# Making the constants out of the weights inside the first scan instead of ahead of the program

## The chip, the core and the metric

The kernel runs on one core of a Trainium2 chip. The core has five engines that run side by side, each through its own list of instructions in order: TensorE (PE, matmuls, with weight loads shown apart as PEld), VectorE (DVE), ScalarE (ACT), GpSimd (POOL) and SyncE (SP), which here only issues transfers. Transfers (DMAs) are issued from SP's queue and from ScalarE's queue and are moved by 16 DMA engines. The metric is the device time of one execution in microseconds (us); less is better. The time before is 4182.01 us, the median of 3 runs (4180.69 to 4185.67).

## The reference, cut to what matters

The input is `x`, 32 sequences of 256 tokens of 256 features. First a conditional state-space block, then two layers of local attention with a gated feed-forward, and the input is added at the end:

```python
xr, gate = split(x @ W_in.T, 2);  xr = xr + t_emb
xc = silu(causal_conv_4_taps(xr) + b_conv)                # 512 channels
xn = layernorm(xc) * ln_g + ln_b
Bm, Cm, dt = split(xn @ W_xproj.T, 3)                     # 16 states each
dt = tanh(dt @ W_dt.T + b_dt) * 0.01
Ad = 1 - dt * tanh(A_log);  Bd = Bm * minimum(norm(xn), 1)
# over the 256 tokens, one after the other:
h = clip(h * Ad + Bd (x) xn, -10, 10);  y = Cm . h
s = ((y + D * xn) * silu(gate)) @ W_out.T
# two layers, windows of 128 tokens, 8 heads of 64:
q, k = rotary(l2norm(q) * q_scale), rotary(l2norm(k) * k_scale)
s = s + attention(q, k, v) @ wo;  s = s + (a * gelu(g)) @ w2
out = x + s
```

Some constants depend on weights alone and not on `x`: the product of `W_dt` with the last third of `W_xproj`, that matrix times `ln_g`, sums of it over the channels (with `ln_g` and with `ln_b`, so that the layernorm can be applied after the projection), the rotary tables times `q_scale` and `k_scale`, half of `W_out`, `-0.01 * tanh(A_log)`, and small selection tables. A flag, `bounded`, says whether the largest `q_scale * k_scale` is so small that the softmax needs no maximum.

## The kernel before

The 32 sequences are worked in 4 groups of 8. `group_scan` is the state-space block of one group: 8 chunks of 32 tokens. Of a chunk it loads `xg`, projects it (`ps_in`, L330), adds the condition into `xr` (L360), applies the taps (`acc`, first on GpSimd at L366, the others on VectorE at L377) and the silu (`th` on ScalarE, L382, and `xc`, L387); projects to the states (`ps_raw`, L396, with `wx_sb`), transposes to tokens on the partitions (`tp_x`, L426), takes the layernorm's statistics (L436 to L446, with a power on GpSimd, L441), multiplies by `lng_sb` and adds `lnb_sb` on GpSimd (L457, L458), writes the rows to `xnd` in HBM (L462), and reads them back spread over the partitions (`xrep`, L547; for the first group half of them instead through `xq`, L602, and matmuls `bx`, L555). ScalarE scales them by `beta` (L566), and VectorE does one custom operation for each token, the recurrence `h` (L573). TensorE reads the states out (`y`, L585); then skip, gate, the projection with `w_out_sb` (L661), and the result goes to `ys` in HBM.

Every piece of this is put on an agenda by step: `at(s, piece, ...)`, where step `32*c + t` is token `t` of chunk `c`, and pieces of work ahead have smaller or negative steps. The order of emission follows the agenda; a scheduler in the framework may then move instructions within an engine's list by its own costs, unless one is marked to be kept in program order. A tile is taken from a pool by its tag, with a number of buffers; a new tile of a tag waits until the readers of the one that had the buffer are done.

`program` runs the scan of group 0 alone, then for each group the attention and feed-forward blocks of both layers, side by side with the scan of the next group. Its text is compiled twice, for both values of the flag; every engine loads `bounded` (L1318) and branches into one of them.

Ahead of the branch stands the setup. It is where the change works: all loads of constants on ScalarE's queue (L112, L119; only `w_in_sb` is on SP's), identity and masks, the halving of `w_out_sb` (L172), `head_rows` (L197), the tables `rc_sb` and `rs_sb` (L229), the flag (L237 to L244), the folding of `W_dt` into `wx` (`td`, `wdT`, L258 to L263), `wx_sb` (L265), and six times a `wide` copy on VectorE (L269) with four matmuls into `tw` (L272), whose sums are `wsum` and `wbias` (L279, L280).

## Time and profile before

| | us |
|---|---|
| median of 3 runs | 4182.01 |
| the profiled execution's own time | 4183.47 |
| its span in the profile | 4181.7 |
| TensorE busy | 3874.3 (93%) |
| VectorE busy | 2619.7 (63%) |
| ScalarE busy | 1742.8 (42%) |
| GpSimd busy | 1708.1 (41%) |

| stretch, us | what runs | length | TensorE | VectorE | ScalarE | GpSimd |
|---|---|---|---|---|---|---|
| 0 to 22.8 | loads, setup up to the flag | 22.80 | 1.55 | 6.58 | 1.49 | 3.31 |
| 22.8 to 37.2 | the rest of the setup | 14.40 | 12.43 | 4.33 | 0.00 | 0.28 |
| 37.2 to 70.7 | first chunk, up to the first `h` | 33.50 | 18.68 | 16.75 | 6.59 | 14.68 |
| 70.7 to 460 | the scan of group 0 alone | 389.30 | 367.77 | 326.23 | 210.07 | 142.74 |

The columns on the right are busy time in the stretch. A line of the timeline reads: start, duration, engine, line of the kernel, operation, the tile written, an arrow to the tiles read, shapes and types, how many records; in brackets how long the engine had been idle and what released it. SPq and ACTq are issues of transfers, not the transfers. A line of waits reads: engine and line that waited, for what, total us, how often, the longest. A float32 matmul leaves two records. A line of busy time by stretch reads: the stretch, its length, then PE, PEld, DVE, ACT and POOL busy with the number of instructions, the granted TensorE clock, DMA share and GB/s. TensorE's busy time is modelled at its ends, and a busy TensorE need not be at its peak.

### The profile page before, as it was taken

To read this page: it belongs to the slowest core of one execution; us is meant where nothing else is said; L and a number is where in the kernel's file an instruction comes from. 1 tells how busy PE (TensorE), PEld (TensorE's weight loads), DVE (VectorE), ACT (ScalarE), POOL (GpSimd) and SP (SyncE) were. 2 spreads that over 40 slices of the span, in tenths; PEclk is the share of its full clock that TensorE was granted. 3 is DMA by queue.
4 is the path that set the end of the run, shared out by engine and by line. 5 is a ranking of instruction groups with operands and counts; after the bars stand their busy time and mean duration, and the time that the engine had idled before them with its cause. 6 is when DMAs were issued, how large, how long until landed. Compare 5 with 4: busy or idle time off the path is not lost. (4 is left out here: it accounts for less than half of the span.)

```text
span 4181.7 us, 51837 instructions
## 1 busy us (share of the span) xinstructions
PE 3874.3 (93%) x18236; PEld 2002.1 (48%) x18236; DVE 2619.7 (63%) x4986; ACT 1742.8 (42%) x3217; POOL 1708.1 (41%) x1749
## 2 busy tenths in 40 slices
PE   6999899899988999899998999989998899999999
PEld 3333355444544455444455445544454545654653
DVE  5888467677766456766867636776776644434443
ACT  2555344444444334444544424444444533322331
POOL 3443265225543156423654136522454315513531
PEclk9999899999999999999999999999999999999999
DMA  3444213444335212344434421344433521000000
GB/s 123 121 124 119 58 44 95 113 117 112 91 87 139 81 43 77 111 110 111 116 86 114 121 65 44 81 126 111 118 91 84 142 78 37 3 19 22 1 11 31
DMA packets 257345, 353.09 MB, mean 84 GB/s; under 512 B 160867, under 2 KB 170420, under 8 KB 254900
## 3 DMA queue, kind: packets, MB, share of 16 engines
q1 hardware_dynamic: 172624, 337.67, 29.0%
q10 hardware_dynamic: 84452, 12.01, 1.8%
q8 instruction: 147, 2.41, 0.2%
q14 instruction: 122, 1.00, 0.1%
HBM read 314.49 MB, written 33.55 MB: 83 GB/s over the span
## 5 line engine op out<-in xcount | busy, mean ns | idle before, releaser
L573 DVE CUSTOM_DVE_ANT_0 h<-h,xrep,lim 128x512 f32<-128x512 f32 x1024 | 908.1, 887 | 94.8 <-PE y L585 36.0
L566 ACT ACTIVATE xrep<-xrep,beta 128x512 f32<-128x512 f32 x896 | 608.6, 716 | 793.3 <-DMA xrep<-xnd 732.8
L781 PE MATMUL ps_qkv<-wqkv_sb,res 128*128 128x512 f32 x1536 | 740.5, 621 | 28.4 <-ACT qT L825 6.6
L805 POOL TENSOR_TENSOR rot<-rot,swp 128x512 f32<-128x512 f32 x256 | 329.2, 1286 | 653.3 <-DVE swp L802 603.3
L781 PEld LDWEIGHTS ps_qkv<-wqkv_sb,res 128*128 128x128 f32 x1536 | 286.6, 196 | 381.9 <-issue 309.0
L813 POOL TENSOR_TENSOR rn<-ss,neg_half 128x8 f32<-128x8 f32 x256 | 437.4, 1708 | 21.6 <-DVE ss L811 9.7
L797 DVE TENSOR_TENSOR rot<-ps_qkv,rc_sb 128x512 f32<-128x512 f32 x256 | 175.6, 686 | 375.6 <-ACT sq L794 375.4
L330 PE MATMUL ps_in<-xg,w_in_sb 128*128 128x256 f32 x1024 | 398.4, 523 | 6.5 <-ACT pT L995 3.4
L1140 PE MATMUL po_f<-ag,w_sb 128*128 128x512 f32 (+1 forms) x768 | 356.0, 612 | 18.5 <-DVE ag L1121 18.5
L585 PE MATMUL y<-h,ly 128*32 128x512 f32 x2048 | 354.0, 639 | 11.3 <-DVE h L573 10.1
L1111 PE MATMUL pa<-hT,w_sb 128*128 128x512 f32 (+1 forms) x896 | 363.0, 595 | 0.0
L1121 DVE SCALAR_TENSOR_TENSOR ag<-pa,b_sb,gl 128x512 f32<-128x512 f32 x192 | 143.5, 747 | 317.9 <-PE pa L1111 166.2
L1111 PE MATMUL pg<-hT,w_sb 128*128 128x512 f32 x640 | 309.4, 606 | 0.0
L330 PEld LDWEIGHTS ps_in<-xg,w_in_sb 128*128 128x128 f32 x1024 | 194.1, 204 | 206.5 <-issue 125.2
L814 POOL TENSOR_TENSOR rot<-rot,rn 128x512 f32<-128x512 f32 x256 | 280.3, 1095 | 19.0
L377 DVE SCALAR_TENSOR_TENSOR acc<-xr,wc_sb,acc 128x256 f32<-128x256 f32 x384 | 199.2, 523 | 116.7 <-POOL acc L366 114.2
L1074 POOL TENSOR_TENSOR rstd<-ve,neg_half 128x1 f32<-128x1 f32 x128 | 75.8, 592 | 476.6 <-DVE ve L1072 466.1
L995 ACT ACTIVATE pT<-sc 128x512 f32<-128x512 f32 x384 | 206.3, 592 | 127.3 <-PE sc L986 113.7
L831 PE MATMUL ps_wo<-oT,wo_sb 128*128 128x256 f32 x1024 | 237.3, 385 | 0.0
L1140 PEld LDWEIGHTS po_f<-ag,w_sb 128*128 128x128 f32 (+1 forms) x768 | 135.1, 190 | 203.3 <-issue 138.7
L794 ACT ACTIVATE sq<-ps_qkv 128x512 f32<-128x512 f32 x256 | 148.8, 593 | 195.9 <-PE ps_qkv L781 148.1
L1111 PEld LDWEIGHTS pa<-hT,w_sb 128*128 128x128 f32 (+1 forms) x896 | 135.6, 170 | 189.3 <-issue 175.7
(151 smaller groups left out, 5592.9 us busy)
## 6 DMA issues: line engine op xcount, KB each, us to landing
xrep<-xnd SPq DMA_DIRECT2D x448, 512.0 KB
xnd<-xn SPq DMA_DIRECT2D x64, 256.0 KB
wqkv_sb<-in_wqkv_dram SPq DMA_DIRECT2D x8, 1536.0 KB
xd<-xnd SPq DMA_DIRECT2D x192, 64.0 KB
w_sb<-in_w_dram SPq DMA_DIRECT2D x8, 1364.0 KB
xg<-in_xT_dram SPq DMA_DIRECT2D x64, 128.0 KB
ys<-yo ACTq DMA_DIRECT2D x64, 128.0 KB
res<-ys SPq DMA_DIRECT2D x32, 256.0 KB
```

The source lines that it names most:

```text
L330: nc.tensor.matmul(ps, w_in_sb[:, k, ch * P : (ch + 1) * P], x, start=(k == 0), stop=(k == KM - 1),)
L566: nc.scalar.activation(bx, ck[c].pop(("bx", t), bx), AF.Copy, scale=ck[c]["beta"][:, t : t + 1])
L573: nc.vector._custom_dve(TENSOR_ADD_SAT, out=h_new, in0=state["h"], in1=bx, s0=ck[c]["lim"][:, 0, t : t + 1], s1=ck[c]["lim"][:, 1, t : t + 1],
L585: nc.tensor.matmul(ck[c]["y", hb][32 * q : 32 * q + 32, :], ly[hb % 2][:, 32 * t : 32 * t + 32], ck[c].pop(("h", hb * TB + t)), start=(i = ...
L781: nc.tensor.matmul(ps, res[b // 2][:, k, b % 2, t0 : t0 + W], wqkv_sb[:, k, a * DI : (a + 1) * DI], start=(k == 0), stop=(k == KM - 1),)
L805: nc.gpsimd.tensor_add(rot, rot, swp)
L813: nc.gpsimd.tensor_tensor(rn, ss, neg_half, ALU.pow)
L814: nc.gpsimd.tensor_mul(rot, rot, bc(rn, 2, DH))
L831: nc.tensor.matmul(po[:, d], wo_sb[:, c, d * P : (d + 1) * P], oT[:, c, :], start=(c == 0), stop=(c == NC_ - 1),)
L995: nc.scalar.activation(p, banks[r], AF.Exp)
L1111: nc.tensor.matmul(ps[0:n, :], self.w1[:, k, half_ * HID + o : half_ * HID + o + n], self.h[j][:, k].rearrange("p b t -> p (b t)"), start= ...
L1140: nc.tensor.matmul(self.po[d], self.w2[r0 : r0 + n, m, d * P : (d + 1) * P], self.ag[m][r0 : r0 + n, :], start=(m == 0), stop=(m == len(MC ...
```

## The change

The flag is computed first of all, from a load on SP's queue. The other constants made of weights go into `constants`, which `group_scan` calls for group 0 and which puts them on the agenda: the folding at steps -43 to -14, later loads at -16, the halving of `w_out_sb` at 14, tables from 50 on, `head_rows` from 100 on. The six `wide` copies, the halving, the tables (now four operations in place of eight) and `head_rows` are on GpSimd instead of VectorE, each marked to be kept at its place in program order. Temporary tiles come from the tags `rot` and `swp` of attention, and PSUM banks from the program's own pool. Both compiled programs contain them.

```diff
@@ -119,18 +119,26 @@
         nc.scalar.dma_start(out=t, in_=src)
         return t
+    bounded = const.tile([1, 1], I32, tag="bounded", name="bounded")
+    with tc.tile_pool(name="setup", bufs=1) as setup:
+        sq = setup.tile([1, L, 2, DH], FP, tag="sq", name="sq")
+        nc.sync.dma_start(out=sq, in_=qk_scale.unsqueeze(0))
+        nc.vector.tensor_mul(sq, sq, sq)
+        big = setup.tile([1, L, 2], FP, tag="big", name="big")
+        nc.vector.tensor_reduce(big, sq, AX.X, ALU.max)
+        nc.vector.tensor_mul(big[:, :, 0], big[:, :, 0], big[:, :, 1])
+        nc.vector.tensor_scalar(big[:, :, 1], big[:, :, 0], SCALES2, None, ALU.is_le)
+        allb = setup.tile([1, 1], FP, tag="allb", name="allb")
+        nc.vector.tensor_reduce(allb, big[:, :, 1], AX.X, ALU.min)
+        nc.vector.tensor_copy(bounded, allb)
     w_in_sb = loaded(w_inT, [P, KM, 2 * DI], "w_in_sb", nc.sync)
     cond_sb = loaded(condT, [P, NC_, B], "cond_sb")
     wc_sb = loaded(w_conv, [P, NC_, TAPS], "wc_sb")
     bconv_sb = loaded(b_conv, [P, NC_], "bconv_sb")
     lng_sb = loaded(s_ln_g.partition_broadcast(P), [P, DI], "lng_sb")
     lnb_sb = loaded(s_ln_b.partition_broadcast(P), [P, DI], "lnb_sb")
-    dskip_sb = loaded(d_skip.partition_broadcast(P), [P, DI], "dskip_sb")
-    w_out_sb = loaded(w_outT, [P, NC_, DM], "w_out_sb")
-    flg_sb = loaded(f_ln_g, [P, L, KM], "flg_sb")
-    flb_sb = loaded(f_ln_b, [P, L, KM], "flb_sb")
-    b1_sb = loaded(b1, [P, L, 2, len(MCH)], "b1_sb")
-    b2_sb = loaded(b2, [P, L, KM], "b2_sb")
     bdt_sb = per_state(b_dt, "bdt_sb")
     a_sb = per_state(a_log, "a_sb")
 
@@ -163,13 +171,6 @@
     nc.gpsimd.memset(neg_half, -0.5)
     half = const.tile([P, NJ], FP, tag="half", name="half")
     nc.gpsimd.memset(half, 0.5)
-    nc.scalar.activation(a_sb, a_sb, AF.Tanh)
-    nc.vector.tensor_scalar(a_sb, a_sb, -1.0, 0.01, ALU.mult, ALU.mult)
-    nc.vector.tensor_scalar(w_out_sb, w_out_sb, 0.5, None, ALU.mult)
 
@@ -192,19 +193,6 @@
     head_rows = const.tile([P, HEADS, DH], FP, tag="head_rows", name="head_rows")
     for r in range(2):
         nc.gpsimd.memset(head_cols[:, r, r * 16 : (r + 1) * 16], 1.0)
-    for h in range(HEADS):
-        row = 32 * (h // 2) + 16 * (h % 2)
-        nc.vector.tensor_copy(
-            head_rows[:, h, :], ident[:, row : row + 1].broadcast_to([P, DH])
-        )
...
     rc_sb = const.tile([P, L, NW, 2, DH], FP, tag="rc_sb", name="rc_sb")
     rs_sb = const.tile([P, L, NW, 2, DH], FP, tag="rs_sb", name="rs_sb")
 
@@ -213,71 +201,14 @@
 
     wsum = const.tile([P, 3], FP, tag="wsum", name="wsum")
     wbias = const.tile([P, 3], FP, tag="wbias", name="wbias")
-    with tc.tile_pool(name="setup", bufs=2) as setup, tc.tile_pool(
-        name="setup_ps", bufs=2, space=PSUM
-    ) as sps:
...
-        wx0 = setup.tile([P, NC_, 3 * NS], FP, tag="wx0", name="wx0")
-        nc.scalar.dma_start(out=wx0, in_=w_xT)
...
-        for c in range(NC_):
-            td = sps.tile([P, P], FP, tag="td", name="td")
-            nc.tensor.transpose(td[0:NS, :], wx0[:, c, 2 * NS : 3 * NS], ident)
-            wdT = setup.tile([NS, P], FP, tag="wdT", name="wdT")
-            nc.vector.tensor_copy(wdT, td[0:NS, :])
-            td2 = sps.tile([P, P], FP, tag="td", name="td2")
-            nc.tensor.matmul(td2[:, 0:NS], wdT, wdt_sb, start=True, stop=True)
-            nc.vector.tensor_copy(wx0[:, c, 2 * NS : 3 * NS], td2[:, 0:NS])
-        nc.gpsimd.memset(wx_sb, 0.0)
-        nc.vector.tensor_mul(wx_sb[:, :, 0 : 3 * NS], wx0, bc(gcol, 2, 3 * NS))
-        for i in range(3):
-            for src, k, dst in ((wx_sb, 0, wsum), (wx0, 1, wbias)):
-                wide = setup.tile([P, NC_, NS, GB], FP, tag="wide", name="wide")
-                nc.vector.tensor_copy(wide, bc(src[:, :, i * NS : (i + 1) * NS], 3, GB))
-                tw = sps.tile([P, 2], FP, tag="tw", name="tw")
-                for c in range(NC_):
-                    nc.tensor.matmul(
-                        tw,
-                        wide[:, c].rearrange("p n b -> p (n b)"),
-                        cols[:, c, :],
-                        start=(c == 0),
-                        stop=(c == NC_ - 1),
-                    )
-                nc.vector.tensor_copy(dst[:, i : i + 1], tw[:, k : k + 1])
-        nc.vector.tensor_add(wbias[:, 2:3], wbias[:, 2:3], bdt_sb)
+    dskip_sb = const.tile([P, DI], FP, tag="dskip_sb", name="dskip_sb")
+    w_out_sb = const.tile([P, NC_, DM], FP, tag="w_out_sb", name="w_out_sb")
+    flg_sb = const.tile([P, L, KM], FP, tag="flg_sb", name="flg_sb")
+    flb_sb = const.tile([P, L, KM], FP, tag="flb_sb", name="flb_sb")
+    b1_sb = const.tile([P, L, 2, len(MCH)], FP, tag="b1_sb", name="b1_sb")
+    b2_sb = const.tile([P, L, KM], FP, tag="b2_sb", name="b2_sb")
+    b1g_sb = const.tile([P, L], FP, tag="b1g_sb", name="b1g_sb")
 
@@ -301,6 +232,148 @@
 
         def bank(pool, tag, name):
             return pool.tile([P, DI], FP, tag=tag, name=name)
+        def constants(at):
+            tmp = {}
+            def work(tag, name, bufs):
+                return ap_.tile([P, HEADS, DH], FP, tag=tag, name=name, bufs=bufs).rearrange(
+                    "p h d -> p (h d)"
+                )
+            def load_w():
+                w = work("rot", "wx", 4)
+                n = NC_ * 3 * NS
+                tmp["wx"] = w[:, 0:n].rearrange("p (c n) -> p c n", c=NC_)
+                tmp["g"] = w[:, n : n + NC_]
+                tmp["cols"] = w[:, n + NC_ : n + 3 * NC_].rearrange("p (k c) -> p c k", k=2)
+                tmp["dt"] = w[0:NS, n + 4 * NC_ : n + 4 * NC_ + NS]
+                nc.scalar.dma_start(out=tmp["wx"], in_=w_xT)
+                nc.scalar.dma_start(out=tmp["dt"], in_=w_dtT)
+                nc.scalar.dma_start(out=tmp["g"], in_=s_ln_g.rearrange("(c p) -> p c", p=P))
+                nc.scalar.dma_start(
+                    out=tmp["cols"][:, :, 1], in_=s_ln_b.rearrange("(c p) -> p c", p=P)
+                )
+                nc.gpsimd.memset(tmp["cols"][:, :, 0], 1.0)
+                nc.gpsimd.memset(wx_sb, 0.0)
+            def fold_1():
+                td = bank(ps_w, "w", "td")
+                for c in range(NC_):
+                    nc.tensor.transpose(
+                        td[0:NS, c * P : (c + 1) * P], tmp["wx"][:, c, 2 * NS :], ident
+                    )
+                wdT = work("swp", "wdT", 3)
+                nc.vector.tensor_copy(wdT[0:NS], td[0:NS])
+                tmp["wdT"] = wdT
+            def fold_2():
+                td = bank(ps_w, "w", "td2")[:, 0 : NC_ * NS].rearrange(
+                    "p (c n) -> p c n", c=NC_
+                )
+                for c in range(NC_):
+                    nc.tensor.matmul(
+                        td[:, c], tmp["wdT"][0:NS, c * P : (c + 1) * P], tmp["dt"],
+                        start=True, stop=True,
+                    )
+                wx = tmp["wx"]
+                nc.vector.tensor_copy(wx[:, :, 2 * NS :], td)
+                nc.vector.tensor_mul(wx_sb[:, :, 0 : 3 * NS], wx, bc(tmp["g"], 2, 3 * NS))
+            def widen_w(i, k):
+                t = ap_.tile([P, NC_, NS, GB], FP, tag="swp", name="wide", bufs=3)
+                src = (wx_sb, tmp["wx"])[k]
+                tc.keep_in_program_order(
+                    nc.gpsimd.tensor_copy(t, bc(src[:, :, i * NS : (i + 1) * NS], 3, GB))
+                )
+                tmp["wide"] = t
+            def sum_w(i, k):
+                if (i, k) == (0, 0):
+                    tmp["tw"] = bank(ps_w, "w", "tw")[:, 0:12].rearrange(
+                        "p (i k n) -> p i k n", i=3, k=2
+                    )
+                t = tmp.pop("wide")
+                for c in range(NC_):
+                    nc.tensor.matmul(
+                        tmp["tw"][:, i, k],
+                        t[:, c].rearrange("p n b -> p (n b)"),
+                        tmp["cols"][:, c, :],
+                        start=(c == 0),
+                        stop=(c == NC_ - 1),
+                    )
+            def sums_w():
+                nc.vector.tensor_copy(wsum, tmp["tw"][:, :, 0, 0])
+                nc.vector.tensor_copy(wbias, tmp["tw"][:, :, 1, 1])
+                nc.vector.tensor_add(wbias[:, 2:3], wbias[:, 2:3], bdt_sb)
+            def decay_rate():
+                nc.scalar.activation(a_sb, a_sb, AF.Tanh)
+                nc.vector.tensor_scalar(a_sb, a_sb, -1.0, 0.01, ALU.mult, ALU.mult)
+            def load_later():
+                for t, src in (
+                    (dskip_sb, d_skip.partition_broadcast(P)), (w_out_sb, w_outT),
+                    (flg_sb, f_ln_g), (flb_sb, f_ln_b), (b1_sb, b1), (b2_sb, b2),
+                    (b1g_sb[DH : DH + MREM], b1[0:MREM, :, 1, len(MCH) - 1]),
+                ):
+                    nc.scalar.dma_start(out=t, in_=src)
+            def halve():
+                tc.keep_in_program_order(
+                    nc.gpsimd.tensor_scalar_mul(w_out_sb, w_out_sb, 0.5)
+                )
+            def load_tables():
+                tab, sc = work("swp", "tab", 3), work("swp", "qk_sc", 3)
+                tmp["tab"] = tab.rearrange("p (i w n) -> p i w n", i=2, w=NW)
+                tmp["sc"] = sc.rearrange("p (i l n) -> p i l n", i=2, l=L)
+                for i, (src, pos) in enumerate(((qk_scale, rot_c), (qk_scale_sw, rot_s))):
+                    nc.scalar.dma_start(
+                        out=tmp["tab"][:, i], in_=pos.rearrange("p w a d -> p w (a d)")
+                    )
+                    for l in range(L):
+                        nc.scalar.dma_start(
+                            out=tmp["sc"][:, i, l],
+                            in_=src[l].rearrange("a d -> (a d)").partition_broadcast(P),
+                        )
+            def tables(i, l):
+                dst = (rc_sb, rs_sb)[i][:, l].rearrange("p w a d -> p w (a d)")
+                tc.keep_in_program_order(
+                    nc.gpsimd.tensor_mul(dst, tmp["tab"][:, i], bc(tmp["sc"][:, i, l], 1, NW))
+                )
+            def head_table(h):
+                row = 32 * (h // 2) + 16 * (h % 2)
+                tc.keep_in_program_order(
+                    nc.gpsimd.tensor_copy(
+                        head_rows[:, h, :], ident[:, row : row + 1].broadcast_to([P, DH])
+                    )
+                )
+            at(-43, load_w)
+            at(-34, fold_1)
+            at(-32, fold_2)
+            for n in range(6):
+                at(-28 + 2 * n, widen_w, n // 2, n % 2)
+                at(-27 + 2 * n, sum_w, n // 2, n % 2)
+            at(-14, sums_w)
+            at(-19, decay_rate)
+            at(-16, load_later)
+            at(14, halve)
+            at(30, load_tables)
+            for n in range(2 * L):
+                at(50 + 6 * n, tables, n // L, n % L)
+            for h in range(HEADS):
+                at(100 + 2 * h, head_table, h)
 
         def group_scan(g, ys):
 
@@ -699,6 +772,7 @@
             at(-1, start)
             if alone:
                 at(-30, spread_weights)
+                constants(at)
             for c in range(NCH):
                 for t in range(CH):
                     at(c * CH + t, step, c, t)
```

## The prediction

> **What bounds the kernel now.** I read the timeline of the first 75 us, then the waits, then busy time by stage. The timeline shows what stands between the launch and the first project-in matmul:
>
> ```profile
> 11.98 0.69 DVE L172 TENSOR_SCALAR w_out_sb<-w_out_sb 128x1024 f32<-128x1024 f32 x1 [11.98 <-DMA w_out_sb<-in_w_outT_dram]
> ...
> 21.99 0.13 DVE L244 CAST bounded<-allb 1x1 int32<-1x1 f32 x1
> ...
> 22.79 2.71 SPq L343 DMA_DIRECT2D xg<-in_xT_dram  x4
> ...
> 26.94 10.37 PE L272 MATMUL tw<-cols,wide 128*128 128x2 f32 x48 [1.23 <-issue]
> ...
> 37.17 6.41 PE L330 MATMUL ps_in<-xg,w_in_sb 128*128 128x256 f32 x16
> ```
>
> VectorE's first instruction waits 12 us for the last big constant; the flag `bounded`, which every engine loads before its branch, is ready at 22.12; the first input slice `xg` is issued only then (0.67 us after); and TensorE, in order, turns to `ps_in` when the 48 `tw` records are through, at 37.17. The waits of SP's queue say the same: it stood 21.4 us at the flag.
>
> ```profile
> SPq L1318 <- DVE wdT L260: 21.4, 1, 21.4
> ```
>
> From 37.17 to the first recurrence step `h` at 70.73 runs one chain: convolution on VectorE, `tp_x`, statistics, then GpSimd's affine pairs, the write of `xnd`, its read back as `xq`, `bx`, scaling.
>
> ```profile
> 54.09 1.08 POOL L441 TENSOR_TENSOR stat<-ve,neg_half 128x1 f32<-128x1 f32 x2 [4.61 <-DVE ve L440]
> ...
> 57.14 1.26 POOL L458 TENSOR_TENSOR xn<-xn,lnb_sb 128x512 f32<-128x512 f32 x1
> 58.36 1.26 POOL L457 TENSOR_TENSOR xn<-xn,lng_sb 128x512 f32<-128x512 f32 x1
> ...
> 59.70 1.26 POOL L458 TENSOR_TENSOR xn<-xn,lnb_sb 128x512 f32<-128x512 f32 x1
> ...
> 63.06 2.68 SPq L602 DMA_DIRECT2D xq<-xnd  x4
> ...
> 70.73 0.80 DVE L573 CUSTOM_DVE_ANT_0 h<-h,xrep,lim 128x512 f32<-128x512 f32 x1
> ```
>
> Two facts follow. GpSimd idles 4.61 us before the first power, so there is room for early work; from 55.80 to 60.96 it is the chain itself. The scan of the first group then runs alone until about 460, a recurrence of 256 steps of about 1.47 us (34 `h` in each 50 us), VectorE 87 to 89% busy. Nothing of attention can start before its end, and attention and feed-forward fill TensorE to the end of the span. So a microsecond saved ahead of the first `h` is saved at the end, unless the lone scan gives it back.
>
> **The change, part by part, in us against the profiled execution (span 4181.7; its time of 4183.47 is 1.8 more; the median of the runs, 4182.0, stands 1.5 under that).**
>
> *The flag first.* Its load is now first on SP's queue, ahead of `w_in`. A load here lands about 2.5 after its issue (`wx`: issued 17.35, used 19.89), so at about 3.2. The six small VectorE operations take 0.41+0.41+0.15+0.15+0.14+0.13, with gaps about 1.55: flag at 4.8, `xg` issued at 5.4. The first 256 KB of `xg` need two issues (1.4) and a landing (about 1.8), some 8.6. `w_in` is there: in 10.5 us the queues now land 2.4 MB, of which 0.77 MB (`dskip`, `w_out`) go later. First `ps_in` at **9.0** (8.3 to 11.5) in place of 37.17: **-28.2**.
>
> *What leaves the setup* (w_out's halving 0.69, tables 8 x 0.25, head rows 0.90, folding, 48 `tw`) is inside these 28.2; it counts once.
>
> *The folding, now in the chain.* In the built order VectorE gets one `wdT` copy (16x512, 0.42 by the 128x512 copy), one `wx` copy (0.2) and `wx_sb` (0.36) among its convolution operations: 1.0. TensorE gets four `td` transposes after three of the four `ps_in` channels, and `td2` after the fourth; the `wx` copy waits for `td2` and VectorE's remaining convolution queues behind it: another 0.8. The last `xc` is late by **+1.8**.
>
> *Six `wide` copies on GpSimd* (VectorE took 0.42 for one). No row has this copy on GpSimd. Nearest: `acc` 128x256 with one tensor input 0.56, doubled 1.12; two-input 128x512 at 1.26 is the ceiling, VectorE's 0.42 the floor. A rule against this move stands in the Trainium skill's page GPSIMD Engine Reference (Elementwise, side-by-side cycle accounting): ordinary elementwise work belongs on VectorE; GpSimd's best loop is given as about 768 ns for 512 elements. I take 1.0, near the row. Four sit ahead of the first power, in the 4.61 idle; but TensorE, in order, has their `tw` groups (four groups of 0.87) ahead of the last `tp_x`, and they compete with VectorE's `acc`: +1.2. `wide` five stands between the two powers and delays the first affine by 0.4 net; `wide` six stands between the pairs: +1.0. Together **+2.6**. By the page's 0.77 it would be +2.0, by 1.26 +3.5. The `tw` of the last `wide` and the three `wsum`/`wbias` operations end under the second affine pair (2.5).
>
> *ScalarE's issues.* After the branch it issues four loads (1.9), loads its table (1.28), does the tanh, then seven loads: in before these took 3.22 to 12.08 with `bdt` and `a` among them and a gap of 2.1 after `w_out`. It is free at about 15.2 (13 to 18.5); the first `th`, 6.85 behind the first `ps_in`, wants it at 15.8. **+0.3** (0 to 2.7). The table loads issued between the `sq_x` take some 2.2, under the 3.1 that ScalarE idles before `ad`. The weights (4.2 MB behind `xg` on SP's queue) now land at 9 to 20 instead of 26 to 39; `xnd` is first written well after.
>
> *GpSimd inside the lone scan, held at its place.* Halving `w_out`, 128x1024: 4 x 0.56 = 2.2, between the two norm halves of the second chunk; four tables of 128x256, half of 1.26 each: 2.6; eight head rows at 0.25 (the 128x24 copy takes 0.20 to 0.36): 2.0. Sum 6.8. GpSimd has idle time (22 busy in 50), so its own share would cost nothing; but the rows say more:
>
> ```profile
> 90.99 1.75 POOL L457 TENSOR_TENSOR xn<-xn,lng_sb 128x512 f32<-128x512 f32 x1 [2.28 <-ACT xn L450]
> ...
> 91.74 1.55 DVE L573 CUSTOM_DVE_ANT_0 h<-h,xrep,lim 128x512 f32<-128x512 f32 x1
> ```
>
> An `h` of 0.80 lasts 1.55 beside a GpSimd operation. The page SBUF — State Buffer (two separate sides) names a cause: VectorE with two SBUF inputs and GpSimd take one port pair exclusively, the loser waiting for the whole instruction; this speaks against the change. With no such contention the 6.8 would cost nothing; with the rule strictly, all 6.8 could fall on VectorE. `h` fills 29 of 50 us, so I charge 0.55: **+3.7** (0 to 7). In this is also the wait of the second `stat`: VectorE holds it behind the halving, with the `h` steps queued after it, about 2.
>
> Nothing else moves: after the first chunk's reshuffled order and GpSimd's 13 insertions, the built sequences agree.
>
> Sum: -28.2 + 1.8 + 2.6 + 0.3 + 3.7 = **-19.8**; span 4161.9, execution 4163.7, median **4162.2**.
>
> **The rivals.**
>
> *B, the scan hides GpSimd's work.* VectorE idles 12% of the scan, so a delay of an `h` can be made up. Then -28.2 + 1.8 + 2.6 + 0.3 = -23.5: 4158.5, and with cheap `wide` copies or an earlier `xg`, down to 4151. Against it: the recurrence is serial on VectorE.
>
> *C, the fold sits on the chain.* `xg`, in pieces of 128 bytes, moved at about 140 GB/s in before, and ScalarE's loads now compete with it; with the first `ps_in` at 11.5, `wide` at 1.26, ScalarE late by 2.7 and all 6.8 paid: -25.7 + 1.8 + 3.5 + 2.7 + 6.8 = -10.9, thus 4171. Its end laps into no measurable change.
>
> *D, the change does not bring the start forward.* If something other than the flag held `ps_in` (`w_in`, say), little is gained: 4178. Against it: SP's 21.4 us wait, and `tw` ending where `ps_in` begins.
>
> *E, slower.* TensorE's granted clock. From 405 to 435 it stood at 0.50 though TensorE showed busy throughout:
>
> ```profile
> 415.00:420.00 5.00, 5.00 (x7) 0.87 (x8) 2.22 (x3) 1.33 (x2) 0.41 (x1) 0.50 0.01 2
> ```
>
> Between 400 and 440 there were 23 `h` where the scan's pace gives 27: four steps, 6 us. If the stalls behind the halving or the tables let the clock drop and it stays down, each us there loses 0.15. To pass from -19.8 to slower by 8.4 it must stay at half through 28.2/0.15 = 190 us more of the scan; below that the change wins. For it: the clock also dipped at 300 to 320 and 340 to 360. Against it: those dips passed within 10 us. Held for 210 us more it gives 4194.
>
> **How the numbers follow.** Chances: forecast 0.62 (its own range 4156 to 4168), B 0.17, C 0.14, D 0.04, E 0.03. 0.2% is 8.4 us, about what a measurement here can tell from no change. Faster by more, under 4173.6: forecast, B and most of C, 0.90; within it: the rest of C and D, 0.07; slower: E, 0.03. The range 4151 to 4172 takes in B's low end and nearly all of C, and leaves out D, E and the tails, under 2 in 10.
>
> **What would show it.** First `ps_in` at 8.3 to 11.5; first `h` at 46 to 50 (forecast 47.2); `wide` copies at 0.8 to 1.3; `lnb_sb`'s second end some 4.4 later, counted from `ps_in`, than in before; the scan's end 18 to 24 earlier; stretched `h` beside the halving and the tables. Wrong would be: a first `ps_in` after 15, a scan longer by over 8, or a stage after the scan whose length changes.

## The result, and the profile after

| | before | after |
|---|---|---|
| median, us | 4182.47 (4179.05 to 4186.25, 6 runs) | 4164.00 (4157.59 to 4168.89, 6 runs) |
| the profiled execution's own time, and its span | 4183.47, 4181.7 | 4163.45, 4161.5 |
| first `xg` issued | 22.79 | 6.26 |
| first `ps_in` | 37.17 | 10.48 |
| first `h` | 70.73 | 51.99 |
| recurrence step 224 | 411.6 | 396.0 |
| last step of the first group's scan, 255 | 462.8 | 435.2 |

The ratio is 0.9956, with a 95% interval of 0.9944 to 0.9968: the change makes the kernel 18.5 us faster, where 19.8 under the profiled execution was forecast, 4162.2 as the median. A second timing gave 4151.52 (5 runs) against 4171.11 (16 runs), ratio 0.995 (0.9936 to 0.9963).

The timeline of the first 52 us of the changed kernel (start, duration, engine, line, operation, in brackets the idle time before and what ended it):

```profile
3.82 0.14 DVE L134 CAST bounded<-allb 1x1 int32<-1x1 f32 x1
...
6.26 3.70 SPq L416 DMA_DIRECT2D xg<-in_xT_dram  x4
...
10.48 4.94 PE L403 MATMUL ps_in<-xg,w_in_sb 128*128 128x256 f32 x12 [10.48 <-DMA xg<-in_xT_dram]
...
22.39 0.61 POOL L289 COPY wide<-wx_sb 128x512 f32<-128x512 f32 x1
22.95 0.80 POOL L289 COPY wide<-wx 128x512 f32<-128x512 f32 x1
23.05 1.86 PE L300 MATMUL tw<-wx,wide 128*128 128x2 f32 x8 [3.41 <-POOL wide L289]
...
27.60 1.26 PE L300 MATMUL tw<-wx,wide 128*128 128x2 f32 x8
28.72 0.53 PE L499 MATMUL tp_x<-ident,xc 128*128 128x128 f32 x3
29.08 1.84 PE L300 MATMUL tw<-wx,wide 128*128 128x2 f32 x16
30.78 0.52 PE L499 MATMUL tp_x<-ident,xc 128*128 128x128 f32 x3
32.10 0.69 PE L499 MATMUL tp_x<-ident,xc 128*128 128x128 f32 x2
32.61 1.30 DVE L509 BATCH_NORM_STATS2 st<-tp_x 128x6 f32<-128x512 f32 x2 [6.36 <-PE tp_x L499]
...
38.89 0.61 POOL L289 COPY wide<-wx 128x512 f32<-128x512 f32 x1
...
51.99 0.89 DVE L646 CUSTOM_DVE_ANT_0 h<-h,xrep,lim 128x512 f32<-128x512 f32 x1
```

The flag is ready at 3.96 and TensorE now waits for `xg`, no longer for the 48 `tw` records. But between the last `xc` (26.26) and the statistics VectorE idles 6.36 us: the `tw` groups stand among the transposes `tp_x` in TensorE's list. A `tw` group is 8 records, not 4. At a granted clock of 0.50 its records follow each other every 0.21 us (1.86 us for the group at 23.05), at 1.00 every 0.11 (1.84 us for the two groups at 29.08). The busy time by stretch shows where the clock was which (the number behind the instructions of the five engines is the granted clock):

```profile
21.20:28.00 6.80, 4.95 (x16) 3.38 (x17) 4.02 (x7) 0.83 (x2) 4.08 (x8) 0.50 0.95 338
28.00:31.50 3.50, 3.50 (x30) 3.26 (x31) 0.00 (x0) 0.00 (x0) 0.00 (x0) 0.99 0.33 130
31.50:48.50 17.00, 9.27 (x32) 7.22 (x30) 5.14 (x21) 3.60 (x8) 8.61 (x11) 0.50 0.24 72
415.00:420.00 5.00, 5.00 (x20) 1.68 (x19) 3.36 (x6) 3.67 (x8) 0.00 (x0) 1.00 0.27 75
```

TensorE has half its clock for 23.9 of the 41.5 us of the first chunk. The last line answers the one shown of before, where the same 5 us had the clock at 0.50: in this execution the end of the scan ran at full clock.

The granted clock does not tell TensorE's pace everywhere. In before the `tw` records also follow each other every 0.21 us, as at half clock, and the view has the clock at 1.00:

```profile
30.00:40.00 10.00, 10.00 (x42) 9.46 (x42) 3.20 (x12) 0.00 (x0) 0.28 (x4) 1.00 0.82 335
```

Within the first `ps_in`, the distance of the records falls from 0.43 to 0.21 us at about 42.6 in before and 14.4 in after, with the clock at 1.00 all along. Early in the kernel the pace must be read from the distance of the records.

The waits of SP's queue, up to 60 us, say why `xg` was issued only at 6.26:

```profile
SPq L1392 <- DVE bounded L134: 2.5, 1, 2.5
...
SPq L416 <- DMA bdt_sb<-in_b_dt_dram: 1.7, 1, 1.7
SPq L416 <- DMA wc_sb<-in_w_conv_dram: 1.7, 1, 1.7
```

The wait of 21.4 us at the flag is 2.5; behind it stand two waits of 1.7 for loads that `xg` doesn't use, ahead of the first and the third of its four issues.

### The profile page after: what moved, and what is told of

The parts are those of the page before. It is cut to its first block, busy times and chain, and to the rows that moved or that the text cites. A ratio compares the mean times of both kernels' runs of the same rounds, so it can differ in the third digit from the quotient of the medians.

```text
span 4161.5 us, 51805 instructions
## 1 busy us (share of the span) xinstructions
PE 3856.3 (93%) x18236; PEld 1997.9 (48%) x18236; DVE 2615.3 (63%) x4953; ACT 1741.2 (42%) x3217; POOL 1718.5 (41%) x1768
## 3 DMA queue, kind: packets, MB, share of 16 engines
q14 instruction: 123, 1.01, 0.1%
## 4 chain that ended last, share of the span: by engine, by line
PE 30%; DVE 7%; DMA 5%; POOL 4%; issue 2%; ACT 2%; SPq 0%; ACTq 0%; POOLq 0%; DVEq 0%
PE ps_qkv L855 6%; PE pa L1185 4%; PE po_f L1214 4%; DMA xrep<-xnd 4%; PE pg L1185 3%; PE ps_wo L905 2%; DVE h L646 2%; PE sc L1060 2%; PE ov L1098 2%; PE ps_in L403 2%; POOL rn L887 1%; PE rs L1079 1%; PE y L658 1%; PE rb L1113 1%; POOL rot L888 1%
## 5 line engine op out<-in xcount | busy, mean ns | idle before, releaser
L403 PE MATMUL ps_in<-xg,w_in_sb 128*128 128x256 f32 x1024 | 399.6, 525 | 17.8 <-DMA xg<-in_xT_dram 10.5
L1214 PE MATMUL po_f<-ag,w_sb 128*128 128x512 f32 (+1 forms) x768 | 356.2, 615 | 18.3 <-DVE ag L1195 18.3
L658 PE MATMUL y<-h,ly 128*32 128x512 f32 x2048 | 343.0, 630 | 12.7 <-DVE h L646 11.0
L1060 PE MATMUL sc<-qT,kT 64*128 64x128 f32 (+1 forms) x2048 | 226.3, 351 | 2.1 <-ACT kT L899 1.8
```

The lines of the kernel that those rows point to most:

```text
L403: nc.tensor.matmul(ps, w_in_sb[:, k, ch * P : (ch + 1) * P], x, start=(k == 0), stop=(k == KM - 1),)
L658: nc.tensor.matmul(ck[c]["y", hb][32 * q : 32 * q + 32, :], ly[hb % 2][:, 32 * t : 32 * t + 32], ck[c].pop(("h", hb * TB + t)), start=(i = ...
L1060: nc.tensor.matmul(banks[r][:, i, :], kT[rows, i0 + i, kw * W : (kw + 1) * W], qT[rows, i0 + i, kw * W :], start=False, stop=(i == n - 1),)
L1214: nc.tensor.matmul(self.po[d], self.w2[r0 : r0 + n, m, d * P : (d + 1) * P], self.ag[m][r0 : r0 + n, :], start=(m == 0), stop=(m == len(MC ...
```

## Where the time went, in two traces of before and three of after

The profile pair differs by 20.2 us of span, near the forecast. Two more traces show that this is partly chance. All in us; where a plus sign stands, counted from the first `ps_in`:

| | before | before, again | after | after, again | after, timed again |
|---|---|---|---|---|---|
| first `ps_in` | 37.17 | 37.07 | 10.48 | 10.28 | 10.81 |
| last `xc` ends | +12.94 | +12.94 | +15.78 | +15.87 | +15.87 |
| first statistics | +15.27 | +15.27 | +22.13 | +25.26 | +25.26 |
| `lnb_sb`'s second end | +23.79 | +23.79 | +31.58 | +34.71 | +34.72 |
| first `h` | +33.56 | +33.47 | +41.51 | +44.05 | +44.74 |
| steps 0 to 224 | 340.8 | 341.0 | 344.0 | 342.5 | 340.5 |
| steps 224 to 240 | 33.9 | 29.1 | 21.4 | 29.0 | 29.0 |
| half clock in these 16 steps | 23.6 | 12.9 | 0.0 | 11.8 | 13.0 |
| last step of the scan to the end of the span | 3718.9 | 3715.9 | 3726.2 | 3716.3 | 3707.1 |

Up to step 224 after is ahead by 15.6, 14.7 and 15.5 us. The steps 224 to 240 then take 21.4, 29 or 34 us; TensorE is busy throughout in all five traces, and they are the longer the more of them its clock was halved. That moved 12.5 us to after in the profile pair. 7.9 of it came back by the end (20.2 of span is left of 28.1 at step 240), and 7.3 of these behind the scan: there after's first trace is the slowest of the five, at 218 us of half clock against 220 in before, so the clock doesn't explain that part. The three traces of after alone lie 19 us apart behind the scan.

## The experiments

**Before and after once more**, without an edit.

> The kernel before, looked at once more, for the granted clock at the end of the lone scan. In the first profile TensorE stood at half clock from 405 to 437 us and the recurrence lost about 12 us there against the kernel after. Theory S (the half-clock stretch belongs to the order of this kernel): it is there again, between step 224 and 240 of the recurrence, 20 us or longer. Theory L (luck of one execution): in this look it is under 10 us or elsewhere, and the first to the last step takes about 382 to 388 us instead of 392.

> The kernel after, looked at once more, for the same stretch. In its first profile the lone scan took 383.2 us from first to last step with no half-clock stretch over 7 us after 52 us. Theory S: again 380 to 386. Theory L: it can as well be 390 or more. Start of the first project-in matmul 10.5 and first recurrence step 52.0 again, within 0.5, by both.

Measured 4176.14 and 4161.58, a distance of 14.6 between two single executions (19 others of before, timed beside them, lie between 4158.79 and 4180.08). Steps 224 to 240 took 29.1 and 29.0: the 12.5 us of the profile pair belong to these two executions, not to the change.

**The flag alone.** The kernel before, with the flag's load and its six VectorE operations first, and the rest of the setup where it was:

```diff
+    with tc.tile_pool(name="setup0", bufs=1) as setup:
+        sq = setup.tile([1, L, 2, DH], FP, tag="sq", name="sq")
+        nc.sync.dma_start(out=sq, in_=qk_scale.unsqueeze(0))
...
+        nc.vector.tensor_copy(bounded, allb)
...
-        sq = setup.tile([1, L, 2, DH], FP, tag="sq", name="sq")
-        nc.scalar.dma_start(out=sq, in_=qk_scale.unsqueeze(0))
...
-        nc.vector.tensor_copy(bounded, allb)
```

> The kernel before with one part of the change alone: the flag's load and its six small operations go first, all other constants stay ahead of the branch on the engines where they were. My theory (the in-order list of TensorE holds the start: the tw matmuls stand ahead of ps_in, and they wait for the loads on ScalarE's queue): ps_in starts at 33 to 37 us, time 4178 to 4184, no measurable gain. Rival (the flag alone holds the start, since SP waited 21.4 us for it): ps_in starts at 15 to 22 us and the time falls by 15 or more, to about 4165.

Measured 4170.80 (12 runs), ratio 1.0004 (0.9994 to 1.0014): nothing won. Its timeline:

```profile
3.55 0.14 DVE L133 CAST bounded<-allb 1x1 int32<-1x1 f32 x1
15.95 5.28 SPq L344 DMA_DIRECT2D xg<-in_xT_dram  x4
...
28.27 10.37 PE L273 MATMUL tw<-cols,wide 128*128 128x2 f32 x48 [1.23 <-issue]
38.51 5.95 PE L331 MATMUL ps_in<-xg,w_in_sb 128*128 128x256 f32 x16
```

The flag came 18 us sooner and `xg` 7, and `ps_in` still starts when the `tw` records are through, 1.3 us later than in before and behind the 33 to 37 of the expectation. So with the flag early, TensorE's list holds the start. The other half, the folding moved with the flag left late, was not run; in before `xg` was issued only behind the flag, at 22.79, so that both parts are needed for a start at 10.5.

**The sums later.** The changed kernel, with the `tw` matmuls behind the chunk's last transposes, held there, and the first four `wide` copies in buffers of their own, so that none waits for another's `tw`:

```diff
-                t = ap_.tile([P, NC_, NS, GB], FP, tag="swp", name="wide", bufs=3)
+                pool, tag, bufs = (aw, "pT", 6) if i < 2 else (ap_, "swp", 3)
+                t = pool.tile([P, NC_, NS, GB], FP, tag=tag, name="wide", bufs=bufs)
...
-                    nc.tensor.matmul(
+                    tc.keep_in_program_order(nc.tensor.matmul(
...
-                at(-27 + 2 * n, sum_w, n // 2, n % 2)
-            at(-14, sums_w)
+                at(-17 + n // 2, sum_w, n // 2, n % 2)
+            at(-13, sums_w)
```

> The kernel after with the 24 tw matmuls held behind the tp_x transposes of the first chunk, and the wide copies in buffers of their own so that none waits for a tw. My theory (the first chunk is late because four groups of tw, eight records each, stand ahead of the last tp_x on TensorE): first statistics at 28 to 29.5 us instead of 32.6, first recurrence step at 47.5 to 49.5 instead of 52.0, time 3 to 4 us under that of the kernel after. Rival (VectorE's inserted folding and the GpSimd copies make it late, TensorE only waits for them): statistics move by under 1 us and the first step stays at 51 to 52.

> The kernel with the late sums once more, for a second distance to the kernel before. Its first one was a ratio of 0.9924; the changed kernel had 0.9956 and 0.995. If the late sums are what they won in the first chunk (first h 6 to 7 us sooner than the 54 to 56 of two of three traces of the changed kernel): ratio 0.991 to 0.994, first statistics at 28 to 29, first h at 47.5 to 49.5. The rival (the first timing was a lucky one): 0.9945 to 0.996.

Measured 4139.03 (6 runs), ratio 0.9924 (0.9908 to 0.994), and the second time 4137.26 (6 runs), ratio 0.9932 (0.9916 to 0.9948). From the timeline of the first run:

```profile
27.92 0.69 PE L500 MATMUL tp_x<-ident,xc 128*128 128x128 f32 x2
28.40 10.24 PE L301 MATMUL tw<-wx,wide 128*128 128x2 f32 x48
28.43 1.30 DVE L510 BATCH_NORM_STATS2 st<-tp_x 128x6 f32<-128x512 f32 x2 [1.62 <-PE tp_x L500]
...
48.09 0.89 DVE L647 CUSTOM_DVE_ANT_0 h<-h,xrep,lim 128x512 f32<-128x512 f32 x1
```

The last `xc` ends at 26.8 and 26.6 in its two traces (26.2 to 26.7 in the changed kernel); the statistics start 1.6 after it instead of 6.4 to 9.4, and the first `h` is at 48.1 and 48.0 against 52.0, 54.3 and 55.6. So the place of the `tw` groups cost the changed kernel 4 to 7.5 us (the buffers and the order were not tried apart). TensorE's half clock alone is not the cause, for the late sums had it as well:

```profile
20.60:44.50 23.90, 20.57 (x76) 16.34 (x76) 10.02 (x31) 4.44 (x10) 12.65 (x19) 0.50 0.50 169
```

This version beats before; against the changed kernel see the next timing.

**The changed kernel timed again**, to have its distance a second time.

> The changed kernel as it is, timed beside the kernel before once more. In the earlier timing the two medians stood 18.5 us apart (ratio 0.9956), and its traces have the first h at 52 to 54 against 70.5 to 70.8 in before, with 1 to 3 us given back in the scan. So here: ratio 0.9945 to 0.9970, 12 to 23 us under the median of before; if the latter is 4169 again, 4146 to 4157, and 3 to 15 us over the kernel with the late sums. The rival (the late sums won something else too, beyond the first chunk): the changed kernel stands 20 us or more over the late sums, at a ratio of 0.998 or above.

Measured 4151.52 against 4171.11, 19.6 apart: the ratio of 0.995 is as expected, and the late sums' two ratios lie below its interval's lower end of 0.9936 (both their intervals reach into it). Against 0.9956 and 0.995 they are 8 to 13 us better, where the first `h` accounts for 4 to 7.5; the rest stays open. That the late sums are faster than the changed kernel rests on the first `h` of five traces; the two were not timed side by side.

**GpSimd's part of the scan left out.** `w_out` isn't halved, the rotary tables stay at 1 and their loads are gone; the head rows are made in the setup:

```diff
-            at(14, halve)
-            at(30, load_tables)
-            for n in range(2 * L):
-                at(50 + 6 * n, tables, n // L, n % L)
-            for h in range(HEADS):
-                at(100 + 2 * h, head_table, h)
```

> The changed kernel without GpSimd's part in the scan: w_out is not halved and the rotary tables are left at 1 (both left out of the computation), head_rows are made in the setup on VectorE while it waits. My step said that GpSimd's work there costs the scan 3.7 us: from the first h to h 224 it then takes 3 to 5 us less than the 342.5 to 344.0 of the changed kernel, all of it within the chunks that hold the halving (steps 12 to 40) and the tables (48 to 80), and the time is 2 to 5 us lower. The rival (the scan hides it; the difference to before seen in the traces is the clock's and the order's): h 224 within 1.5 us of 342.5 to 344.0, and the same time within 2 us.

Measured 4146.88 (4 runs), ratio 0.9946 (0.9925 to 0.9967), which the time can't tell from after's 0.995. Up to h 224 the scan takes 338.8 us, 1.7 to 5.2 less than in the three traces of after. That alone shows little: the second trace of the late sums has GpSimd's work in it and takes 337.4. The stretches of steps say more. The scan by stretches of steps, with the half-clock time in each in brackets:

| | steps 0 to 12 | 12 to 48 | 48 to 128 |
|---|---|---|---|
| before | 21.0 (3.4) | 53.7 (0.0) | 125.1 (6.8) |
| before, again | 20.9 (3.4) | 53.6 (0.0) | 125.2 (6.8) |
| flag alone | 21.1 (3.4) | 55.7 (6.8) | 125.8 (10.2) |
| scan bare | 18.3 (1.3) | 53.8 (0.0) | 125.7 (13.7) |
| after | 17.2 (0.0) | 56.6 (6.8) | 128.8 (17.1) |
| after, again | 17.2 (0.0) | 55.9 (6.8) | 128.8 (17.1) |
| after, timed again | 17.2 (1.9) | 53.8 (0.0) | 128.2 (13.7) |
| late sums | 18.7 (3.4) | 53.8 (0.0) | 128.3 (13.7) |
| late sums, again | 17.2 (1.7) | 53.8 (0.0) | 126.2 (3.4) |
| wide copies on VectorE (below) | 21.0 (3.4) | 53.6 (0.0) | 127.5 (13.7) |

The halving falls in steps 12 to 48. Where the clock didn't drop there, every kernel of the table takes 53.6 to 53.8, with the halving and without it: in sum it costs nothing. It is not hidden, though. VectorE stands 1.75 us behind it for the second `stat` in four of the traces and 3.20 in one, as the prediction had it, and in these four the `h` beside it last 1.5 and 1.2. In before VectorE stands 2.65 us in the same steps, waiting for TensorE's `y`, and in the bare scan 1.4 and 1.4; a wait for GpSimd takes the place of a wait for TensorE. The tables and head rows fall in steps 48 to 128: at the same half-clock time (13.7) the kernels with them take 127.5, 128.2 and 128.3 against 125.7, that is 1.8 to 2.6 us; in the one trace with little half clock (3.4) 126.2, some 1 us over before at 6.8. Against that, the first 12 steps got 3.8 shorter in after: in before VectorE stood 3.04 us in them, waiting for the second chunk's transposes,

```profile
85.63 0.70 DVE L436 BATCH_NORM_STATS2 st<-tp_x 128x6 f32<-128x512 f32 x1 [3.04 <-PE tp_x L426]
```

and in after the same statistics come without a wait:

```profile
64.41 0.69 DVE L509 BATCH_NORM_STATS2 st<-tp_x 128x6 f32<-128x512 f32 x1
```

Wait and length go together: in the five traces without the wait the 12 steps take 17.2, with 1.4 to 2.2 us of it 18.3 to 20.2, with 2.9 to 3.2 from 20.9 to 21.1. What takes it away was not tested. TensorE's list for the second chunk is in another order in after, but the late sums have the wait in one trace and not in the other, so the order alone doesn't decide it.

**The scan's part on VectorE**: `nc.gpsimd` to `nc.vector` in the halving, the tables and the head rows.

```diff
-                    nc.gpsimd.tensor_mul(dst, tmp["tab"][:, i], bc(tmp["sc"][:, i, l], 1, NW))
+                    nc.vector.tensor_mul(dst, tmp["tab"][:, i], bc(tmp["sc"][:, i, l], 1, NW))
```

> The changed kernel with the halving, the four tables and the eight head_rows on VectorE at the same places in place of GpSimd. On GpSimd the tables and head_rows cost the steps 48 to 128 some 2.7 us (128.2 to 128.8 against 125.7 without them). On VectorE they are 4 x 0.42 and 8 x 0.11, about 2.6, on the engine that the recurrence runs on: steps 48 to 128 take 127 to 128.5 and the time is within 3 us of the changed kernel, if VectorE's idle eighth takes up little. The rival (VectorE's gaps take them, and only the contention with GpSimd costs): 125.5 to 126.5 there, and 2 to 3 us less.

Measured 4145.46 (6 runs), ratio 0.9948 (0.993 to 0.9966), the same as after within the interval; steps 48 to 128 took 126.3 at 6.8 us of half clock, against 125.1 in before at the same: 1.2 us. That lies in the range of the rival (125.5 to 126.5), that VectorE's gaps take them, and not in the 127 to 128.5 expected; the gain of 2 to 3 us that the rival forecast can't be seen in the time. By the tiles' views the operations last, on GpSimd in after,

```profile
L330 POOL TENSOR_SCALAR w_out_sb<-w_out_sb x1: 3207/3207/3207, 72.8 to 72.8; 128x1024 f32<-128x1024 f32 x1
...
L351 POOL TENSOR_TENSOR rc_sb<-tab,qk_sc x2: 731/733/735, 134.2 to 137.8; 128x256 f32<-128x256 f32 x2
...
L357 POOL COPY head_rows<-ident x8: 227/333/703, 207.6 to 235.1; 128x64 f32<-128x64 f32 x8
```

and on VectorE here, for the head rows (a row of a tile's view has the shortest, median and longest in ns, then the first and last start in us)

```profile
L357 DVE COPY head_rows<-ident x8: 160/187/228, 209.5 to 226.6; 128x64 f32<-128x64 f32 x8
```

Whether GpSimd or VectorE is the better place for them stays open: the two kernels were traced at different half-clock times, and the difference is under what the timing tells.

**The wide copies on VectorE**, the same edit in `widen_w`.

> The changed kernel with the six wide copies on VectorE (0.42 each in the kernel before) at the same steps. VectorE has the convolution in hand until its last xc, so the first four copies come behind it, and TensorE has their tw groups ahead of ps_raw and tp_x: first statistics at 35 to 39, first h at 56 to 60, 1 to 5 us over the changed kernel; the affine pairs then run without a copy between them. The rival (GpSimd is the slower place): first h at 50 to 54, time 1 to 4 us lower than the changed kernel.

Measured 4153.09 (7 runs), ratio 0.9969 (0.9953 to 0.9985); against after's 0.995 (0.9936 to 0.9963): the two overlap, and the trace decides. The last `xc` ends 14.68 after the first `ps_in` instead of 15.78 to 15.87, so the copies beside the convolution cost it 1.1 to 1.2, and the folding alone, against before's 12.94, 1.7. The first statistics come 8.67 after that, within the 6.4 to 9.4 of after, but at 33.7, ahead of the 35 to 39 expected. But from there to the second end of `lnb_sb` it takes 13.24 instead of 9.45, since copies five and six and `wsum`, which waits for all `tw`, now stand among VectorE's small operations on the statistics; first `h` at 56.71, in the expected range. By this trace GpSimd is the better place for the six at these steps, by 1.2 to 4.7 us at the first `h`.

**Nothing held at its place**: no call of `keep_in_program_order` in `constants`.

> The changed kernel with nothing held at its place: the scheduler puts the eight head_rows ahead of the first acc, the halving of w_out between the convolution's first taps, where GpSimd has to wait for w_out's load, and the last two wide copies ahead of the first power. If the holding is what makes the move to GpSimd harmless: the first xc of the later channels is late by the wait for w_out (first ps_in at 10.4 as before; last xc 3 to 8 us later, first h at 54 to 60), while the scan up to step 48 is 2 to 4 us shorter; time 0 to 6 us over the changed kernel. The rival (the place doesn't matter, since GpSimd idles enough): first h within 1.5 us of 52 to 54 and the time within 3 us of the changed kernel.

Measured 4153.61 (11 runs), ratio 0.9962 (0.9951 to 0.9974). GpSimd's timeline, ahead of the third channel's first tap:

```profile
20.86 2.78 POOL L333 TENSOR_SCALAR w_out_sb<-w_out_sb 128x1024 f32<-128x1024 f32 x1 [5.04 <-DVE wx L285]
23.88 0.55 POOL L442 TENSOR_SCALAR acc<-xr,wc_sb,bconv_sb 128x256 f32<-128x256 f32 x1
```

GpSimd waits 5.04 and then halves for 2.78, with `acc` behind it. (The profile names the copy into `wx`, which the halving doesn't read; that it was the load of `w_out` is likely and not shown.) Last `xc` at 30.98, 4.3 to 4.8 later, first `h` at 60.08. The scan gives a part back: steps 48 to 128 took 125.8, as in the bare one, since the tables were done before. The saving that I expected in the first 48 steps didn't come. So holding the pieces at their places is worth 4.5 to 8 us at the first `h`, of which 4.3 to 4.8 stand at the last `xc`, behind the halving (the marks were not taken off one by one); in the medians timed together only 2.1 of it shows, which is within their spread.

**Loads reordered, first try**, on top of the late sums: all `wide` copies early, `bdt_sb` and `a_sb` loaded behind `wx`.

```diff
-        nc.scalar.dma_start(out=t, in_=src)
+        later_loads.append((t, src))
...
+                for t, src in later_loads:
+                    nc.scalar.dma_start(out=t, in_=src)
...
-                at(-28 + 2 * n, widen_w, n // 2, n % 2)
+                at(-28 + n, widen_w, n // 2, n % 2)
...
-            at(-13, sums_w)
+            at(-12, sums_w)
```

> The kernel with the late sums, with three edits more: all six wide copies stand ahead of the first power, the loads of b_dt and a_log come behind those of wx, so that SP's queue doesn't wait for them ahead of xg, and wsum and wbias are held behind both stat. By my account of the first chunk: xg issued at 5.0 to 5.5 in place of 6.3, first ps_in at 9.0 to 9.5, first statistics at 26.5 to 28.5, both affine pairs without a copy between them, first h at 45.0 to 47.0 in place of 48.1; time 1 to 4 us under the late sums' own distance to before, ratio 0.989 to 0.993. The rival (ps_in waits for w_in or the first half of xg, whatever issues them): ps_in stays at 10.3 and the first h at 47 or later.

Measured 4148.99 (5 runs), ratio 0.9952 (0.9938 to 0.9966): worse than the late sums. `xg` was issued at 4.63, as expected, and `ps_in` began at 10.23 all the same: what lies ahead in the transfers set it. And ScalarE's waits show two new ones:

```profile
ACT xn L528 <- PE tw L305: 9.0, 1, 9.0
...
ACT th L460 <- issue: 5.3, 1, 5.3
```

The first `th` came at 20.35, behind ScalarE's own issues of the later loads. And the loads of `qk_sc` now stood ahead of `xn` in its list, with their buffers still held by `wide` copies that `tw` was reading: 9.0 us. First `h` at 55.5.

**Loads reordered, second try**: late sums and early copies; `lng` and `lnb` behind `wx`; the tables' loads in buffers of the tag `rot`; head rows in the setup.

```diff
-    lng_sb = loaded(s_ln_g.partition_broadcast(P), [P, DI], "lng_sb")
-    lnb_sb = loaded(s_ln_b.partition_broadcast(P), [P, DI], "lnb_sb")
...
+            at(-42, load_ln)
...
-                tab, sc = work("swp", "tab", 3), work("swp", "qk_sc", 3)
+                tab, sc = work("rot", "tab", 4), work("rot", "qk_sc", 4)
```

> Late sums, and three more edits by what the runs showed: lng and lnb (512 KB) are loaded behind wx and not ahead of xg; all six wide copies stand ahead of the first power; the tables are loaded into buffers that no wide copy uses, so that ScalarE's queue doesn't wait for tw; head_rows are made by VectorE in the setup. If the first xg waits for what is ahead of it in the transfers: xg issued by 5.3, first ps_in at 8.8 to 9.7, first statistics at 26 to 28, lnb's second end 8.5 to 9 behind them, first h at 44.5 to 46.5; steps 48 to 128 take 127 to 127.8 (tables alone on GpSimd); time 2 to 6 us under the late sums, ratio 0.989 to 0.9925. The rival (w_in's 1 MB alone sets ps_in): ps_in at 10.2 or later and first h at 46.5 or later, 0 to 2 us under the late sums.

Measured 4150.55 (22 runs), ratio 0.9958 (0.9948 to 0.9968): no better than the changed kernel, and missed.

```profile
7.91 1.19 PE L412 MATMUL ps_in<-xg,w_in_sb 128*128 128x256 f32 x2 [7.91 <-DMA xg<-in_xT_dram]
...
15.12 1.10 ACTq L334 DMA_DIRECT2D b_sb<-in_b_dram  x2
...
20.39 1.47 ACTq L334 DMA_DIRECT2D b1g_sb<-in_b_dram  x1
...
21.91 0.72 ACT L464 ACTIVATE th<-acc 128x256 f32<-128x256 f32 x2 [12.14 <-DMA flb_sb<-in_f_ln_b_dram]
```

With 512 KB fewer ahead of it, `ps_in` began at 7.91, 2.3 sooner than in the first try, where `xg` was issued at the same 4.63: the transfers ahead of `xg` do set the start. But ScalarE's last issues, which took 10.41 to 16.25 in after, now end at 21.86, and the first `th` waits for them: 21.91, where `ps_in` + 7.1 would be 15.0. All that was won, and more, is lost there: first `h` at 51.88. The transfers on SP's queue behind `xg` (`wqkv`, 1536 KB) are issued at 8.51, shortly before; why an issue on ScalarE's queue stood still for up to 4 us was not tried.

## Why the prediction was right, and where it was not

The total and the sign held, and in the main the mechanism: the start moved by 26.7 of the 28.2, and the loss behind it is in the first chunk and in the scan. But the loss in the first chunk is about twice what was charged, and the sum came out near the measured time in part by luck. Of the signs named, the first `ps_in` came in its range; the first `h` (52.0 to 55.6 for 46 to 50), `lnb_sb`'s second end (7.8 to 10.9 later for 4.4), the `wide` copies (0.61 to 0.80 for 0.8 to 1.3) and the scan's end (27.5 us earlier in the profile pair, 15.2 in the second, for 18 to 24) did not. Step by step:

*The flag first*, -28.2. Measured -26.7 (10.48 for the 9.0). The load landed sooner than I took (`sq` used at 2.02), the flag was ready 0.8 sooner, but `xg` waited 1.7 us at SP for landings of other loads, then for the transfers ahead of it.

*The folding*, +1.8. Measured +2.8 to +2.9. With the copies on VectorE, behind the last `xc`, it is +1.7, so the term was right, and 1.1 is the contention of the first copies with VectorE's `acc` that I had put into the next term.

*Six `wide` copies*, +2.6. This is the term that failed. The copies are cheaper than I took, 0.61 to 0.80 in place of 1.0; the page GPSIMD Engine Reference of the Trainium skill (Elementwise, side-by-side cycle accounting), whose 0.77 I set aside for the row of `acc`, was the nearer one. But I counted four `tw` groups of 0.87. A float32 matmul leaves two records, as my own reading guide said, and the 48 records in 10.37 us that I quoted make six groups of 1.73, at the granted clock of 1.00 that the view of before has there. From the last `xc` to the first `h` the chunk grew by 5.1 us in one trace and by 7.6 to 8.3 in the two others, where TensorE kept half clock through all the groups (in the first it had the full clock in nearly three of them); `wide` six between the affine pairs cost 0.93 of it, as I had said (1.0). The late sums show it: there the way from the last `xc` to the first `h` is 0.7 to 0.9 us longer than in before, which is about `wide` six alone.

*ScalarE's issues*, +0.3 with 2.7 as the far end. Nothing in after; but the cover is thin. The two kernels with reordered loads lost 3.0 and 6.9 us of the first `th` at just this place.

*GpSimd in the lone scan*, +3.7. From the first `h` to step 224 after took 3.2, 1.5 and -0.3 more than before. The tables and head rows cost 1 to 2.6; the halving in sum nothing, though VectorE waits behind it as I had said and I took it for a third of the term; the first 12 steps gained 3.8, of which I had written only that their order is reshuffled; between steps 12 and 48 the two traces with 6.8 us of half clock are 2 to 3 us longer, as is the flag alone, which has no halving there. The port rule that I quoted from the page SBUF, taken strictly, could have put all of GpSimd's work on VectorE. Single `h` did stretch (from 0.80 to between 1.01 and 1.24 beside three of the four tables), but over the stretch the 1 to 2.6 are far from the 6.9 that tables and head rows last on GpSimd.

*The sum.* At step 224 I had -19.8 and the traces have -14.7 to -15.6, between the forecast and rival C's -10.9. The 4 to 5 us are the `tw` term (2.2 to 5.3), the start (1.4 to 1.8) and the copies' contention (1.1), less what the scan cost under 3.7 (0.5 to 4.1). The medians nevertheless stand 18.5 and 19.6 apart. So 3 to 5 us of the medians' distance are in no trace up to step 224. Behind the scan the traces are too far apart to find them: the three traces with the setup ahead (before twice, the flag alone) take 3714.5 to 3718.9 from the last step to the end, the eleven traces of the changed kernel and its variants 3702.2 to 3726.2. Where the 3 to 5 us come from stays open, and with that the forecast's closeness is in part luck: a term that was too small met a distance that no trace accounts for. By the prediction's own sign, a stage after the scan whose length changes, the sum would be wrong: in the profile pair that stage grew by 7.3 us. Three traces of one kernel differ there by 19, so this sign can't tell a right sum from a wrong one.

## What to carry to other kernels

To move work off a serial start, look at each engine's list at the new place: what stands behind the moved instruction there matters more than its own duration. Here six sums, four of them among eight transposes, made the way from the last `xc` to the first `h` 5 to 8 us longer where 2.6 were charged, and behind the transposes under 1. A load that is issued by a computing engine is work of this engine, and here it held the next activation for 3.0 and 6.9 us. When a difference of some 20 us is explained from one pair of traces, take a second pair first: here one stretch of 16 steps differed by 12.5 us between executions.

## What the runs showed of the hardware

- TensorE's granted clock falls to half and back in pieces of 3.41 us or multiples of it, in all 14 traces. In the traces of after it stood at half for 23.9, 30.7 and 34.1 us between 19 and 58 us. Steps 224 to 240 of the scan took 21.4 us with no half clock, 29 with 12 to 13 us of it, and 33.9 with 23.6.
- The granted clock is not yet the pace. `tw` records follow each other every 0.21 us at 0.50 and every 0.11 at 1.00 in after, but every 0.21 at 1.00 in before (27 to 37 us). From 27 us on TensorE was busy there for 15.7 us before the distance of its records halved; in the first trace of after for 4.
- One-input copies of 128x512 float32 took 0.61 to 0.80 us on GpSimd, the longer ones while VectorE worked on the convolution; an `acc` of VectorE beside them took up to 0.94 instead of 0.48.
- `w_out`'s halving (128x1024) took 3.21 on GpSimd within the scan (2.77 in one trace), 2.78 outside of it, and 1.75 on VectorE within the scan, against 0.69 in the setup of before.
- By the view of waits, the first issue of `xg` on SP's queue waited for landings of loads from ScalarE's queue that its transfer doesn't read: 1.7 us in after, 11.6 with the flag alone.
